# Output projection of two heads by plain products, with reciprocals in one transfer and the value exchange on SP

## The chip, the cores and the metric

The kernel runs on one core of a Trainium2 chip. The metric is the device time of one execution in microseconds. Engines are named as in the profile: PE (TensorE's matmuls), PEld (its weight loads), DVE (VectorE), ACT (ScalarE), POOL (GpSimd), and SP (SyncE, which here only issues DMAs).

## The reference

One transformer layer: layer norm, attention of 16 heads of 128 over 2048 tokens of width 256, and a feed-forward part with ternary weights, added up with the input. Cut to what matters:

```python
qkv = einsum('bsd,ed->bse', xn, Wqkv)               # 16 heads of 128, S = 2048, dim = 256
logits = einsum('bqhd,bkhd->bhqk', q, k) * 128 ** -0.5
w = softmax(logits)
out = einsum('bhqk,bkhd->bqhd', w, v).reshape(B, S, H * D)
y = einsum('bse,de->bsd', out, Wout)                # the output projection: all heads summed
x = x + y + ffn(xn)
```

Everything is float32. An fp32 matmul is two instructions in the profile; a product of a 128 x 128 weight with 512 columns is issued in two halves of 64 rows (`in_halves`), so it is four instructions.

## The kernel before, in words

After a lead-in of some 130 us (layer norm, the feed-forward part, first keys, queries and values) the kernel runs over 64 blocks `n`: 16 heads `h`, and for each four blocks `b` of QB = 512 queries. A block has four steps `t`, one for each 128 queries. Heads come in groups `g` of G = 2, so a group has GB = 8 blocks. All instructions of one step are issued in an order written out by hand (the loop from L1031); each engine keeps that order.

In the step of index `u = 4n + t`:

- `scores` (L610) computes the scores of a step `v = u + 6`, that is six steps ahead (16 PE instructions in two PSUM tiles). DVE takes their maxima (L630, L633), ACT the exponentials (L640) into the tiles `p`.
- `exchanged` (L646) sends `p` from SBUF to SBUF, into the tiles `part`, in 16 DMAs: ten are issued by SP, six by ACT (L659). With 32 x 32 transposes on DVE (L706, two steps later, in `transposed`) that turns the exponentials around. The tiles `p` and `part` are few, so an exponential waits for an older exchange to land, and an exchange waits for an older transpose.
- `differences` (L711, L726) forms sums and differences of the turned exponentials on POOL, and `weighted` (L755, L773) multiplies them with the values. Values times exponentials and other products here use seven block products in place of eight (Strassen's scheme), with the extra additions on POOL and DVE. `v_combined` (L742, L748) forms the sums of the values, once a head, on POOL.
- `copied` (ACT, L791) and `added` (DVE, L799) put the result of a block together in `oU`. At the end of a block `added` multiplies `oU` with the reciprocals of the sums into `oT` (L801). `put_away` (L827), the first thing that POOL does in the next block, stores `oT` in DRAM (`ods`).
- The reciprocals come from `inverses` (L664, in step 2 of the block before): sum, reciprocal and a transpose on DVE, then four DMAs on POOL into a row of DRAM (`rds`, L678). `spread` (L682, L685, step 1 of the block) reads that row back into all partitions, in `oT`.

Beside that, products for the other heads and groups are put into the same steps. In steps 2 and 3: keys and queries of a later head (`fast_product`, `fast_read`, L163 to L217, tiles `pw`), and `fast_scaled` (L219), which makes one query block out of a key block by a scaling on DVE (L223), once in two blocks. In steps 0 and 1 of the first four blocks of a group: the output projection of the two heads of the group before (`fast_o_product`, tiles `pow`). In steps 0 and 1 of the last four blocks: the values of the next group (`fast_v_product`, tiles `pvw`). A first product stands behind the scores; when `twice` is set, a second one stands behind the weighting, and DVE reads it at the start of the next step. All these products share one PSUM bank (tag `m`), so each waits until DVE has read the one before.

The projection before takes two query blocks and two heads at a time: `o_fetched` (L834) loads what was put away into `o3`, `o_difference` (L841) forms differences on POOL, `sums_of` the sums of weights, and seven products a pair of blocks are read by DVE into the sums `osums`, each into one to four places (L911). `y_moved` (L837) brings the sums of a block from DRAM (`yds`) and back. `o_moved`, `o_begun` and `o_loaded` say in which block and step each of these stands.

The values of the next group are turned around too: `v_sent` (L317, four DMAs into DRAM, `vds`), `v_landed` (L324, two DMAs back into `v_part`), `v_transposed` (L328, L331, two transposes on DVE). For the first head of the next group `v_sent` stands in step 0 of the sixth and eighth blocks of a group, `v_landed` in step 1, `v_transposed` in step 2; for the second head in steps 2, 3 and, with a step or more between, in the block after. All those DMAs are issued by POOL. `between` (L988) is called at the end of a step, behind that step's exchange, and holds most of this order.

Of the kernel before, what the change touches and what calls it, by code (L numbers as in the profile page):

```python
# [20 lines left out]
def layernorm_attention_bitffn_kernel(  # L21
# [206 lines left out]
    o3 = const.tile([P, 3, QB], F32, tag="o3", name="o3")  # L228
# [88 lines left out]
    def v_sent(h: int, half: int):  # L317
# [3 lines left out]
        for q in range(P // 32):  # L321
            nc.gpsimd.dma_start(vd[q], v[bass.ts(q, 32)].rearrange("r (j c) -> r j c", c=S // 8))

    def v_landed(half: int):  # L324
        for u in range(2):
            nc.gpsimd.dma_start(v_part[u], vds[half][:, bass.ts(u, QB)])

    def v_transposed(h: int, half: int):  # L328
# [335 lines left out]
    def inverses(n: int):  # L664
# [12 lines left out]
        for j in range(P // 32):  # L677
            nc.gpsimd.dma_start(  # L678
                rds[n % 2][:, bass.ts(j, 32)], riT[32 * j : 32 * j + TB, :]
            )  # L680
# [112 lines left out]
    def added(n: int, r: int):  # L793
# [6 lines left out]
        if r == 3 and n < NBK - NB:  # L800
            nc.vector.tensor_tensor(oT, u, rbs[n], ALU.mult)  # L801
# [22 lines left out]
    def put_away(n: int):  # L824

        h, b = blocks[n]
        nc.gpsimd.dma_start(ods[h % (2 * G)][b], oT)  # L827
# [6 lines left out]
    def o_fetched(g: int, pair: int, i: int, head: int, c: int):  # L834
        nc.gpsimd.dma_start(o3[:, i], ods[(g * G + head) % (2 * G)][2 * pair + c])

    def y_moved(pair: int, c: int, back: bool):  # L837
        y, yd = osums[:, c], yds[2 * pair + c]
        nc.gpsimd.dma_start(*((yd, y) if back else (y, yd)))

    def o_difference(i: int, a: int, b: int):  # L841
        nc.gpsimd.tensor_tensor(o3[:, i], o3[:, a], o3[:, b], ALU.subtract)  # L842

    def o_loaded(g: int, i: int):
        if i % 2 == 0:
            y_moved(i // 2, 0, False)

    def o_moved(g: int, i: int, t: int):

        pair, more = i // 2, i == 1  # L850
        at = i % 2, t
        if at == (0, 0):
            o_difference(1, 2, 1)
        elif at == (0, 1):
            o_difference(0, 1, 0)
        elif at == (0, 2):
            o_fetched(g, pair, 2, 1, 0)
        elif at == (1, 0):
            o_difference(2, 2, 1)
            if more:  # L860
                o_fetched(g, 1, 0, 0, 0)
        elif at == (1, 1):
            y_moved(pair, 1, True)
        elif at == (1, 2):
            if more:
                y_moved(1, 1, False)
                o_fetched(g, 1, 1, 0, 1)
            else:
                y_moved(pair, 0, True)
        elif at == (1, 3) and more:  # L870
            y_moved(pair, 0, True)
            o_fetched(g, 1, 2, 1, 1)
            o_difference(1, 1, 0)

    def o_begun(g: int, i: int, t: int):

        at = i, t
        if at == (6, 2):
            o_fetched(g, 0, 0, 0, 0)
        elif at == (6, 3):  # L880
            o_fetched(g, 0, 1, 0, 1)
        elif at == (7, 1):
            o_difference(1, 1, 0)
        elif at == (7, 2):
            o_fetched(g, 0, 2, 1, 1)

        if at == ((6, 3) if g else (7, 2)):
            y_moved(0, 1, False)

    def o_parts(g: int, m: int):  # L890
        w = weights[g, "o"]
        k, q = w[:, :, :P], w[:, :, P:]
        s = wxs[f"wos{g}"]
        k0, k1, q0, q1 = (0, 0), (1, 0), (0, 1), (1, 1)
        return (
            ((s[:, 0], 1, (k1, q1)), (s[:, 3], 2, (k1,))),
            ((k[:, 0], 0, (k1, q1, k0, q0)),),
            ((s[:, 2], 0, (q0, q1)), (k[:, 1], 2, (k0,))),
            ((s[:, 1], 1, (k1, q0, q1)), (q[:, 1], 2, (q0,))),
        )[m % NB]  # L900

    def fast_o_product(g: int, m: int, second: bool):
        lhs, i, _ = o_parts(g, m)[second]
        pm = ps_m.tile([P, QB], F32, tag="m", name=f"pow{g}_{m}_{int(second)}")
        in_halves(pm, lhs, o3[:, i], True, True)
        return pm

    def fast_o_read(g: int, m: int, second: bool, pm):
        for c, e in o_parts(g, m)[second][2]:
            y = osums[:, c, e]  # L910
            nc.vector.tensor_tensor(y, pm, y, ALU.add)  # L911

# [75 lines left out]
    def between(n: int, t: int):  # L988
# [14 lines left out]
        if g and i < NB:  # L1003
            o_moved(g - 1, i, t)
        elif n < last:
            o_begun(g, i, t)
# [4 lines left out]
        if n >= last - 1 and t == (1 if n < last else 2):  # L1011
            b = n + 1 - last
            nc.gpsimd.dma_start(o3[:, b % 2], ods[(H - 2) % (2 * G)][b])
# [189 lines left out]
```

## Time and profile before

| what | before |
|---|---|
| median of 3 runs | 2299.64 us (2299.03 to 2301.24) |
| the profiled execution | 2299.23 us |
| its span, first to last instruction | 2297.5 us, granted TensorE clock 0.992 |
| busy PE / DVE / POOL / ACT | 95% / 82% / 77% / 32% of the span |
| DMA | 398.46 MB, mean 173 GB/s; exchange 2556 issues on SP, 1540 on ACT |
| median from issue to landing | exchange 2.2 us (SP), 2.5 us (ACT); values out 3.6 us, values in 5.2 us (POOL) |

In the groups of the profile a row gives line, engine, operation, tiles and shapes, then the count, the busy time in us and the mean of one in ns, and behind the second bar the idle time of the engine ahead of them and what ended it. In a timeline a row gives the start and the length in us, the engine, the line, the operation, the tiles and the count; brackets give the idle time ahead and what ended it. Rows of SPq and ACTq are issues of DMAs. Matmuls are pipelined: one of 128 x 512 is shown as 594 ns, and the next may start after some 213.

### The profile page before, as it was taken

What the parts mean: (1) busy time and instruction counts of PE and PEld (TensorE: products, weight loads), DVE (VectorE), ACT (ScalarE), POOL (GpSimd) and SP (SyncE); (2) the same over time, 40 slices, a digit from 0 to 9 for tenths busy, and PEclk for the clock granted to TensorE, in tenths of its full rate; (3) what the DMA queues carried; (4) which work ended last, traced back from release to release, by engine and by line L of the source; (5) the groups of instructions that cost most, each with busy time, mean ns of one, the idle gap of its engine ahead of it and who ended that gap; (6) DMA issues with size and microseconds to landing.
All of it is one profiled execution on the core that took longest, in us unless ns stands there. A gap on an engine that the chain in (4) does not pass through costs nothing.

```text
span 2297.5 us, 41411 instructions
## 1 busy us (share of the span) xinstructions
PE 2189.6 (95%) x13514; PEld 1094.3 (48%) x13514; DVE 1887.3 (82%) x2562; ACT 744.9 (32%) x1390; POOL 1765.6 (77%) x1376
## 2 busy tenths in 40 slices
PE   9999999999999999899998999999999999999898
PEld 6744444454445444455444544444444544445455
DVE  6577888888788888789888888888888788888764
ACT  5543332333232323323333233332333233323331
POOL 0167878887788887988788887888789788898773
PEclk9999999999999999999999999999999999999999
DMA  2166667676676767776677766767677676776764
GB/s 89 55 151 155 150 179 196 166 208 158 175 205 173 189 161 190 193 193 184 162 184 187 199 175 174 198 173 191 159 183 210 171 185 161 189 194 184 193 172 123
DMA packets 246568, 398.46 MB, mean 173 GB/s; under 512 B 80720, under 2 KB 85264, under 8 KB 246352
## 3 DMA queue, kind: packets, MB, share of 16 engines
q1 hardware_dynamic: 127664, 174.95, 29.9%
q0 software_dynamic: 43792, 118.93, 18.6%
q10 hardware_dynamic: 74896, 101.94, 17.3%
q8 instruction: 106, 1.74, 0.3%
q14 instruction: 110, 0.90, 0.1%
HBM read 77.66 MB, written 49.41 MB: 55 GB/s over the span
## 4 chain that ended last, share of the span: by engine, by line
PE 28%; POOL 23%; DMA 19%; DVE 14%; issue 7%; SPq 5%; ACT 2%; ACTq 2%; DVEq 0%; POOLq 0%
DMA part<-p 17%; POOL R L726 14%; PE s L94 10%; PE av L773 8%; SPq L659 5%; DVE mx L630 4%; DVE R L706 3%; POOL st L748 2%; PE ph L508 2%; ACTq L659 2%; ACT p L640 2%; PE pow L94 1%; DVE oU L799 1%; PE pvw L94 1%; PE pw L94 1%
## 5 line engine op out<-in xcount | busy, mean ns | idle before, releaser
L726 POOL TENSOR_TENSOR R<-R 128x1024 f32<-128x1024 f32 x441 | 1181.6, 2686 | 37.0 <-DVE R L706 17.1
L640 ACT ACTIVATE p<-s,nm 128x1024 f32<-128x1024 f32 x512 | 566.2, 1111 | 1381.8 <-DMA part<-p 924.0
L94 PE MATMUL s<-kT,qT 128*64 128x512 f32 x4000 | 946.2, 594 | 13.9 <-ACT p L640 13.7
L630 DVE TENSOR_REDUCE mx<-s 128x1 f32<-128x1024 f32 x512 | 613.1, 1218 | 182.3 <-PE s L94 168.1
L706 DVE STREAM_TRANSPOSE R<-part 128x1024 f32<-128x1024 f32 x512 | 605.2, 1220 | 48.4 <-DMA part<-p 44.9
L94 PEld LDWEIGHTS s<-kT,qT 128*64 128x64 f32 x4000 | 331.1, 137 | 529.0 <-issue 442.1
L773 PE MATMUL av<-R,st 128*64 128x256 f32 x3024 | 495.9, 388 | 53.7 <-POOL R L726 50.2
L773 PE MATMUL av<-R,v 128*64 128x256 f32 x3728 | 539.7, 379 | 0.4 <-DVE oU L799 0.3
L773 PEld LDWEIGHTS av<-R,v 128*64 128x64 f32 x3728 | 341.9, 137 | 186.5 <-issue 56.7
L773 PEld LDWEIGHTS av<-R,st 128*64 128x64 f32 x3024 | 297.7, 139 | 208.1 <-POOL R L726 77.4
L678 POOL DMA_DIRECT2D rd<-r x240 | 124.8, 527 | 162.4 <-DVE r L676 162.1
L827 POOL DMA_DIRECT2D od<-oT x60 | 34.5, 575 | 157.7 <-DVE oT L801 150.2
L799 DVE TENSOR_TENSOR oU<-av,oU 64x256 f32<-64x256 f32 x248 | 101.1, 408 | 54.5 <-ACT oU L791 51.9
L911 DVE TENSOR_TENSOR osums<-pow,osums 128x512 f32<-128x512 f32 x196 | 124.6, 677 | 0.6 <-PE pow L94 0.6
L791 ACT COPY oU<-av 64x256 f32<-64x256 f32 x248 | 91.0, 367 | 94.4 <-PE av L773 90.1
L94 PE MATMUL pw<-t,ws 128*64 128x512 f32 x336 | 109.2, 592 | 0.0
L640 ACT ACTIVATION_READ_ACCUMULATOR p<-s,nm 128x1 f32 x512 | 100.2, 196 | 0.0
L160 POOL TENSOR_TENSOR t<-xnT 128x512 f32<-128x512 f32 x4 | 5.1, 1270 | 107.2 <-DMA part<-p 107.2
L315 DVE TENSOR_TENSOR v<-pvw,v 128x512 f32<-128x512 f32 x98 | 65.1, 676 | 24.9 <-PE pvw L94 24.9
L94 PE MATMUL pw<-xnT,wk 128*64 128x512 f32 x224 | 67.5, 599 | 14.2 <-DVE kT L200 14.2
L200 DVE TENSOR_TENSOR kT<-pw,kT 128x512 f32<-128x512 f32 x112 | 76.9, 686 | 1.8
L842 POOL TENSOR_TENSOR o<-o 128x512 f32<-128x512 f32 x56 | 71.7, 1280 | 0.5
(165 smaller groups left out, 1630.8 us busy)
## 6 DMA issues: line engine op xcount, KB each, us to landing
part<-p SPq DMA_DIRECT2D x2556, 64.0 KB, 2.2
part<-p ACTq DMA_DIRECT2D x1540, 64.0 KB, 2.5
oT<-rd POOLq DMA_DIRECT2D x60, 256.0 KB, 4.3
od<-oT POOLq DMA_DIRECT2D x60, 256.0 KB, 3.6
o<-od POOLq DMA_DIRECT2D x60, 256.0 KB, 4.4
vd<-v POOLq DMA_DIRECT2D x112, 128.0 KB, 3.6
xnT<-vd POOLq DMA_DIRECT2D x56, 256.0 KB, 5.2
osums<-yd POOLq DMA_DIRECT2D x28, 512.0 KB, 6.2
```

The source lines that it names most:

```text
L94: nc.tensor.matmul(out[c * HP : (c + 1) * HP], lhs[:, c * HP : (c + 1) * HP], rhs, start=start, stop=stop, skip_group_check=True,)
L200: nc.vector.tensor_tensor(k, pk, base, ALU.add)
L630: nc.vector.tensor_reduce(mx[:, i : i + 1], s, AX.X, ALU.max)
L640: nc.scalar.activation(p, s, AF.Exp, bias=nm, accum_out=sums[n][:, t, i : i + 1],)
L659: queue.dma_start(parts[v][g // 2][bass.ts(j, 32), g % 2, :], ps[j // 2][bass.ts(g, 32), bass.ts(j % 2, S // NQ)],)
L678: nc.gpsimd.dma_start(rds[n % 2][:, bass.ts(j, 32)], riT[32 * j : 32 * j + TB, :])
L706: nc.vector.transpose(to[:, t % 2, 2 * i : 2 * i + 2], part.rearrange("p g (s c) -> p g s c", s=2),)
L726: nc.gpsimd.tensor_tensor(o, x, y, ALU.subtract)
L773: nc.tensor.matmul(av[i * HP : (i + 1) * HP, half], l[:, kk], moving(s, kk), start=start, stop=(k == units[r] - 1), skip_group_check=True,)
L791: nc.scalar.copy(u[op, oq], av[ap, half])
L799: nc.vector.tensor_tensor(u[p, q], av[p, half], u[p, q], ALU.add)
L911: nc.vector.tensor_tensor(y, pm, y, ALU.add)
```

## The change

The output projection is done with plain products: for each query block and each half of the 256 outputs, one product for each of the two heads, both added up in PSUM, and one sum by DVE. No differences and no weight sums are formed for it. A step does one such pair of products behind the scores, and there is no second one behind the weighting. The two heads of a block lie side by side in DRAM and are fetched by one DMA; the sums of one block are brought while those of the other are in work.

The reciprocals go to DRAM in one DMA of the whole transposed tile, and the spread reads four runs of 128 out of it; the order of the reciprocals in a row differs by that, so the multiplication reads them in another order. It now works in place in `oU`, and `put_away` stores `oU`.

`v_sent` and `v_landed` are issued by SP. The scaling in `fast_scaled` is done by ACT.

```diff
@@ fast_scaled
-        nc.vector.tensor_scalar(q0, k1, SCALE, None, ALU.mult)
+        nc.scalar.activation(q0, k1, AF.Copy, scale=SCALE)
...
-    o3 = const.tile([P, 3, QB], F32, tag="o3", name="o3")
+    o3 = const.tile([P, G, QB], F32, tag="o3", name="o3")
@@ v_sent
-            nc.gpsimd.dma_start(vd[q], v[bass.ts(q, 32)].rearrange("r (j c) -> r j c", c=S // 8))
+            nc.sync.dma_start(vd[q], v[bass.ts(q, 32)].rearrange("r (j c) -> r j c", c=S // 8))
@@ v_landed
-            nc.gpsimd.dma_start(v_part[u], vds[half][:, bass.ts(u, QB)])
+            nc.sync.dma_start(v_part[u], vds[half][:, bass.ts(u, QB)])
@@
-        [away.tile([P, QB], F32, tag=f"od{h}_{c}", name=f"od{h}_{c}") for c in range(NB)]
-        for h in range(2 * G)
+        [away.tile([P, G, QB], F32, tag=f"od{g}_{c}", name=f"od{g}_{c}") for c in range(NB)]
+        for g in range(2)
...
-    rds = [away.tile([TB, P], F32, tag=f"rd{i}", name=f"rd{i}") for i in range(2)]
+    rds = [away.tile([P, 32], F32, tag=f"rd{i}", name=f"rd{i}") for i in range(2)]
@@ inverses
-        for j in range(P // 32):
-            nc.gpsimd.dma_start(
-                rds[n % 2][:, bass.ts(j, 32)], riT[32 * j : 32 * j + TB, :]
-            )
+        nc.gpsimd.dma_start(rds[n % 2], riT)
@@ spread
-            nc.gpsimd.dma_start(oT, rds[n % 2].rearrange("t p -> (t p)").partition_broadcast(P))
+            r = rds[n % 2].rearrange("(j c) r -> j (c r)", c=32)[:, : TB * 32]
+            nc.gpsimd.dma_start(
+                oT.rearrange("p (j x) -> p j x", j=P // 32), r.partition_broadcast(P)
+            )
@@ added
-            nc.vector.tensor_tensor(oT, u, rbs[n], ALU.mult)
+            u = u.rearrange("p (t j r) -> p t j r", t=TB, r=32)
+            r = rbs[n].rearrange("p (j t r) -> p t j r", t=TB, r=32)
+            nc.vector.tensor_tensor(u, u, r, ALU.mult)
@@ put_away
-        nc.gpsimd.dma_start(ods[h % (2 * G)][b], oT)
+        nc.gpsimd.dma_start(ods[h // G % 2][b][:, h % G], oU)
@@ o_fetched, o_difference, o_loaded, o_moved, o_begun, o_parts, fast_o_product, fast_o_read go; new:
+    def o_fetched(g: int, b: int):
+        nc.gpsimd.dma_start(o3, ods[g % 2][b])
+
+    def y_moved(b: int, back: bool):
+        y, yd = osums[:, (b + 1) % 2], yds[b]
         nc.gpsimd.dma_start(*((yd, y) if back else (y, yd)))
+
+    def o_product(g: int, m: int, second: bool):
         w = weights[g, "o"]
+        pm = ps_m.tile([P, QB], F32, tag="m", name=f"pow{g}_{m}")
+        for i in range(G):
+            in_halves(pm, w[:, i, bass.ts(m % 2, P)], o3[:, i], i == 0, i == G - 1)
         return pm
+
+    def o_read(g: int, m: int, second: bool, pm):
+        y = osums[:, (m // 2 + 1) % 2, m % 2]
+        nc.vector.tensor_tensor(y, pm, y, ALU.add)
@@ between
         if g and i < NB:
-            o_moved(g - 1, i, t)
-        elif n < last:
-            o_begun(g, i, t)
+            if t == 0 and i + 1 < NB:
+                y_moved(i + 1, False)
+            elif t == 2:
+                y_moved(i, True)
+                if i + 1 < NB:
+                    o_fetched(g - 1, i + 1)
+        elif n < last and (i, t) == (GB - 1, 2):
+            y_moved(0, False)
+            o_fetched(g, 0)
...
-            if i == GB - 1 and n < last:
-                wo = weights[g, "o"]
-                sums_of(wo[:, :, :P], wo[:, :, P:], f"wos{g}")
@@ the loop
-                    product, read, twice = fast_o_product, fast_o_read, j % NB != 1
+                    product, read, twice = o_product, o_read, False
...
-                if n >= GB and n % GB < NB:
-                    o_loaded(n // GB - 1, n % GB)
```

More of the change, by code (lines that the diff above doesn't have):

```diff
@@ L826, in put_away @@
         h, b = blocks[n]
[L827 to L890, printed above, removed]
-        w = weights[g, "o"]
[L892 to L905, printed above, removed]
-        return pm
[L908 to L911, printed above, removed]
+        nc.gpsimd.dma_start(ods[h // G % 2][b][:, h % G], oU)
@@ L1012, in between @@
             b = n + 1 - last
-            nc.gpsimd.dma_start(o3[:, b % 2], ods[(H - 2) % (2 * G)][b])
+            nc.gpsimd.dma_start(o3[:, b % 2], ods[(H - 2) // G % 2][b][:, 0])
         if g and (i, t) == (0, 1):
```

## The prediction

> **What bounds the kernel now.** I read the page first (busy shares, groups, DMA issues), then the waits, then the timelines of PE, POOL, DVE and SP in and between two groups of heads. From the page:
>
> ```profile
> PE 2189.6 (95%) x13514; PEld 1094.3 (48%) x13514; DVE 1887.3 (82%) x2562; ACT 744.9 (32%) x1390; POOL 1765.6 (77%) x1376
> ...
> L678 POOL DMA_DIRECT2D rd<-r x240 | 124.8, 527 | 162.4 <-DVE r L676 162.1
> ...
> L911 DVE TENSOR_TENSOR osums<-pow,osums 128x512 f32<-128x512 f32 x196 | 124.6, 677 | 0.6 <-PE pow L94 0.6
> ...
> L842 POOL TENSOR_TENSOR o<-o 128x512 f32<-128x512 f32 x56 | 71.7, 1280 | 0.5
> ```
>
> PE is the fullest engine. Its timeline in block 41 (the second of a group, with output products in it) shows it running without a hole:
>
> ```profile
> 1535.32 3.60 PE L94 MATMUL s<-kT,qT 128*64 128x512 f32 x16
> 1538.76 1.03 PE L94 MATMUL pow<-o,wos 128*64 128x512 f32 x4
> 1539.61 3.81 PE L773 MATMUL av<-R,st 128*64 128x256 f32 x32
> ```
>
> A product is four instructions; from its start to the next start is 1539.61 - 1538.76 = 0.85 us. Block 40, the first of the group, does have holes, and POOL's timeline there has none for 40 us:
>
> ```profile
> 1501.58 0.59 PE L773 MATMUL av<-R,st 128*64 128x256 f32 x2
> 1505.31 3.10 PE L773 MATMUL av<-R,st 128*64 128x256 f32 x16 [3.13 <-POOL R L726]
> ```
>
> ```profile
> 1493.45 1.13 POOL L326 DMA_DIRECT2D xnT<-vd  x2
> 1494.58 0.56 POOL L827 DMA_DIRECT2D od<-oT  x1
> 1495.12 0.54 POOL L839 DMA_DIRECT2D osums<-yd  x1
> ```
>
> So the loop is PE-bound with a few holes, and I count those by block. From one multiplication L801 to the next in DVE's timeline is a block. The sixes of a group (n = 6 mod 8) last 32.3 us in the median and the second ones 32.6; I take 32.4 as PE's floor. Over it, summed over the seven groups: first blocks 253.8 - 7 x 32.4 = 27.0 us, third blocks 8.6. The sixth blocks of the six whole groups with value products (n = 5 mod 8) have 1.8 each, the eighth 3.1 each. That is what can be won, and where. The last view is DVE at the eighth block's end and SP's queue beside it:
>
> ```profile
> 1755.16 0.71 DVE L331 STREAM_TRANSPOSE v<-xnT 128x512 f32<-128x512 f32 x1 [1.26 <-DMA xnT<-vd]
> 1756.06 0.71 DVE L331 STREAM_TRANSPOSE v<-xnT 128x512 f32<-128x512 f32 x1 [0.18 <-DMA xnT<-vd]
> ```
>
> ```profile
> 1758.29 1.08 PE L94 MATMUL pw<-xnT,wk 128*64 128x512 f32 x4 [1.51 <-DVE kT L200]
> ```
>
> ```profile
> 1198.76 46.46 SPq L659 DMA_DIRECT2D part<-p  x52
> ```
>
> DVE waits for the landed values, and PE waits 1.51 us for DVE's next read behind them: there a microsecond of DVE is a microsecond of PE. SP issues 52 transfers in 46.46 us with no break the view would part.
>
> **The change, part by part.** The sum starts from the profiled execution, 2299.2 us (span 2297.5); the median of the runs, 2299.6, is 0.4 above, and I carry the sum over as it is. About 0.2%, 4.6 us, can be told from no change.
>
> *Products.* Before, 224 + 168 = 392 instructions make 98 products; after, two for each of 8 steps in 7 groups, 112. 14 x 0.855 = **+12.0 us**, all on the path, since PE has no hole where they go (the second step of first and third blocks).
>
> *POOL's and DVE's share of the output.* Gone are 56 differences (71.7 us of POOL), four weight sums a group (0.47 each, 1.9), four fetches a group (0.57 each), and of 196 sums on DVE 140 (140 x 0.677 = 95 us of DVE). Most of this is beside PE. On the path is the chain that starts with put-away L827, which waits for DVE's multiplication (POOL waits 150.2 us for it, 44 times, so in most blocks POOL was early and its relief is worth nothing). In block 40 it was 2.2 us late; without the work before it, it starts 0.3 us after the multiplication's end, at 1492.7. Then 0.56 + 4.82 + 2.52 + 2.35 (put-away, differences, value sums, half of T2; the fetch of y, 0.54, is gone) puts the half at 1502.95 and, with 0.55 for a y load and 2.4, the other half at 1505.9. PE arrives 0.86 later by its extra product and 0.58 earlier without its wait for the first read, at 1501.9: waits of 1.1 and 1.2 where it had 3.5, 1.8 and 0.58. Won: 3.6 us. The same in block 24, where the put-away was on time: 4.2 before, 2.6 left, won 1.6. With four blocks like 24, 48 worse than 40 (5 us) and 56 at 1.3 that is 17 us. In third blocks PE waited 0.6 to 1.5 us for L911; one product and one read a step end that: 7 us. Together **-24** (between -14, if only the excess of blocks 40 and 48 goes, and -36, all of 27.0 + 8.6).
>
> *Reciprocals.* Four issues (4 x 0.527) become one. The nearest row for its 128 pieces is 0.57. The broadcast has four runs a partition now; its issue costs between 0.57 as before and 4 x 0.57; the weight load with two runs took 0.72, so I take about 1. POOL wins a microsecond a block and is early in most: **-3** (0 to -6), in blocks 0 to 7, where it is late at t = 1. The multiplication reads in runs of 32 and now works in place; 0.69 alone before, and the permuted sums L200 take 0.69 too: 0. The nearest permuted row with a longer time is L223, 1.46; 60 x 0.77 = 46 us of DVE would be the other end, but that row is slow for another reason:
>
> *The scaling of q0* leaves DVE (28 x 1.463 = 41 us) for ACT. Its 28 times are 1.29 or 1.60 us but for one of 0.43; POOL's differences run beside the slow ones. [...] By the rows: PE's weight loads waited 13.9 us for L197 behind it, 27 times, most under the 0.4 us of other gaps; I take **-6** (0 to -14). ACT gets 28 x 0.60 (row L132) at the head of a step, waiting for DVE's k sum; the exps are queued behind, and ACT was idle 1381.8 us before exps: hidden.
>
> *oU instead of oT.* ACT's next copy into oU now waits until the put-away has landed. From the multiplication's end to that copy are 5.6 us in the median; the issue comes 0.3 later and lands after 3.65. The margin is negative in 11 of 60 blocks, by 2.0 at most. Behind the copy are six exchange issues and two exps, and PE needs the copy only after 16 score instructions (3.4) and a product: 0; if that cover is gone, +8 (11 blocks by 0.7).
>
> *Values by SP.* 24 issues a group leave POOL (16 x 0.565 and 8 x 0.557) and go behind SP's exchange. Price on SP: 0.42 (its loads at the start) to 0.59 (an exchange issue), so four sends take 1.7 to 2.4 us, and the ten exchange issues of the next step, the two loads and all later exchanges stand behind them. DVE needs the loads one step after, in the sixth and eighth blocks: 14 places. POOL issued them on average 4.0 us before SP ended the exchange of that step (0.4 to 8.8 us in the 14). So SP's loads start 4.0 + 1.9 = 5.9 later. They land faster: 5.2 now by POOL, 2.2 for an exchange piece of 64 KB by SP; I take 3.2, so 2.0 is won back. And the ten issues, which took 6.4 us in calm steps and up to 12.4 here, no longer share the engines with the loads: I take 1.9. Left: 2.0 us a place, and PE's wait grows with it: **+28**. Ends: -15 (DVE's present waits at L331, 10.3 + 4.7, go) and 14 x 3.9 = +55 (nothing won from sharing). [...]
>
> Sum: 12 - 24 - 3 - 6 + 28 = +7, so **2306 us**.
>
> **The rivals.** *SP has room* (faster). SP's own waits include 100.3 us for DVE's transposes L706, 87 times: there it is ahead, as with 2.7 us just before the exchange at 1687. If the sends fall into such gaps and contention takes the rest, the values cost 3 us instead of 28: 12 - 24 - 3 - 6 + 3 = -18, 2281. It decides below 1.5 us a place, where the other terms' -21 is used up (21 / 14). Against it: DVE waits for these loads already.
> *SP becomes the bound.* 12 more issues in the sixth and eighth blocks at 0.59 are 7.1 us, of which its gaps take about 3.0; 14 x 4.1 = 57 in place of 28: +36, 2335. For it: exchange groups there already follow each other after 0.1 us in most steps. Against: transposes have 2 to 8 us between landing and use.
> *They cancel*: within 4.6 us, 2299. The parts do what they say: nothing suggests that a part is without effect on the program.
>
> **How the numbers follow.** Slower as summed 0.42, SP as the bound 0.12, SP with room 0.38, cancelling 0.08. Slower is 0.42 + 0.12 = 0.54. The range: the faster case spreads from 2264 to 2294, the bound one from 2320 to 2355; leaving out the lowest fifth of the one and most of the other's upper half gives 2270 to 2334. The summed case alone is 2304 to 2318.
>
> **What would show it.** Right: pow at 448 instructions with a matmul time near 0.594 each; L911's successor 56 times; PE's waits for POOL R halved in first blocks (about 2.4 us each left); blocks of first and third kind near 34.8 and 33.4; DVE's wait at the value transposes (now 15 us) near 40, with PE's pw wait for DVE kT grown by as much; sixth and eighth blocks longer by 2. Wrong: value waits on DVE unchanged or less (then SP had room), exps late and PE's scores waiting for ACT (then SP is the bound), or ACT's copies waiting for put-aways while PE waits for them (the oU cover was not there).

## The result, and the profile after

The changed kernel takes 2478.12 us in the median of 4 runs (2460.64 to 2481.69), the kernel before 2300.14 beside it: a ratio of 1.0763, with a 95% interval from 1.0724 to 1.0802. The prediction was 2306. The side was right and the size was not: 178 us more, where 7 were forecast. The profiled execution took 2478.82 us (span 2477.0, granted clock 0.958 where it was 0.992).

First the page of the changed kernel, its busy line and groups (before: PE 2189.6, POOL 1765.6; 240 stores of reciprocals, 196 sums):

```profile
PE 2224.6 (90%) x13570; PEld 1088.2 (44%) x13570; DVE 1776.7 (72%) x2394; ACT 762.8 (31%) x1418; POOL 1491.8 (60%) x916
...
L677 POOL DMA_DIRECT2D rd<-r x60 | 33.5, 559 | 256.4 <-DVE r L676 256.4
L331 DVE STREAM_TRANSPOSE v<-xnT 128x512 f32<-128x512 f32 x56 | 37.4, 692 | 134.5 <-DMA xnT<-vd 95.9
...
L94 PE MATMUL pow<-o,wo 128*64 128x512 f32 x448 | 105.6, 592 | 0.2 <-DVE qT L197 0.2
```

What the change meant to do, it did: 448 product instructions, 60 stores, POOL relieved by 274 us and DVE by 111 us. But the value transposes L331, whose waits were 15 us, now wait 134.5, and PE is idle where it was not. The waits of PE, with the total, the number and the longest:

```profile
PE pw L94 <- DVE kT L200: 146.5, 25, 13.3
PE pw L94 <- DVE qT L197: 41.9, 14, 6.3
PE s L94 <- ACT p L640: 28.6, 17, 5.9
PE av L773 <- POOL R L726: 20.3, 21, 3.1
```

Before, the same four were:

```profile
PE av L773 <- POOL R L726: 50.2, 41, 4.1
PE pw L94 <- DVE kT L200: 14.2, 13, 3.1
PE s L94 <- ACT p L640: 13.7, 11, 6.1
PE pw L94 <- DVE qT L197: 1.1, 4, 0.6
```

So POOL's lateness went down by 30 us, as meant, and two new waits of 132 and 41 us came. They have their places. The length of a block, from multiplication to multiplication (L801 before, L803 after), is the mean over the blocks 8 to 59:

| block of the group | 1 | 2 | 3 | 4 | 5 | 6 | 7 | 8 |
|---|---|---|---|---|---|---|---|---|
| before, us | 36.3 | 33.1 | 33.6 | 33.3 | 34.5 | 34.2 | 32.2 | 35.5 |
| after, us | 37.2 | 37.2 | 36.1 | 35.2 | 34.0 | 39.6 | 33.5 | 45.1 |

The sixth and eighth blocks, those with the value exchange, take most of it: 109 of the 183 us by which the blocks n = 1 to 59 got longer. One eighth block end in the timelines of SP, DVE and PE:

```profile
984.96 10.10 SPq L659 DMA_DIRECT2D part<-p  x15
995.10 7.03 SPq L322 DMA_DIRECT2D vd<-v  x4
1002.30 9.88 SPq L659 DMA_DIRECT2D part<-p  x10
1012.23 1.08 SPq L326 DMA_DIRECT2D xnT<-vd  x2
1013.47 4.95 SPq L659 DMA_DIRECT2D part<-p  x8
```

```profile
1015.34 1.35 DVE L331 STREAM_TRANSPOSE v<-xnT 128x512 f32<-128x512 f32 x2 [11.89 <-DMA xnT<-vd]
...
1017.46 0.69 DVE L200 TENSOR_TENSOR kT<-pw,kT 128x512 f32<-128x512 f32 x1
```

```profile
1002.73 3.60 PE L94 MATMUL s<-kT,qT 128*64 128x512 f32 x16
1018.21 1.97 PE L94 MATMUL pw<-xnT,wk 128*64 128x512 f32 x4 [11.88 <-DVE kT L200]
```

Read from the top: the four sends take SP 7.03 us (1.7 to 2.4 were forecast), the ten exchange issues of the next step start behind them and take 9.88, the loads are issued at 1012.23. DVE stands idle for 11.89 us at the transposes. PE's next product needs the PSUM bank that DVE's read L200 frees, which stands behind them: 11.88 us. And that product then takes 1.97 us instead of 1.08. The reason for that is in the windows of the same stretch (columns: window, length, PE's busy time and count, granted clock, DMA share, GB/s):

```profile
1000.00:1005.00 5.00, 5.00 (x36) 1.00 0.99 285
1005.00:1010.00 5.00, 1.33 (x8) 0.92 0.85 250
1010.00:1015.00 5.00, 0.00 (x0) 0.50 0.66 182
1015.00:1020.00 5.00, 1.79 (x6) 0.50 0.50 132
1020.00:1025.00 5.00, 5.00 (x28) 0.72 0.59 145
```

The granted clock is 0.50 in the window in which PE is idle throughout and in the one after it; PE works again from 1018.21, and in the last window the clock is still 0.72 in the mean. So the stall costs more than its length here: PE's busy time grew by 35.0 us (2224.6 - 2189.6), and only 12 of these, by the prediction's estimate, are the added products.

The second stall, DVE's wait for the scaling, is seen at the end of a third block, in ACT's, DVE's and PE's timelines:

```profile
827.71 6.50 ACTq L659 DMA_DIRECT2D part<-p  x6
834.26 0.63 ACT L223 ACTIVATE qT<-kT 128x512 f32<-128x512 f32 x1 [10.53 <-DMA part<-p]
```

```profile
834.93 0.69 DVE L197 SCALAR_TENSOR_TENSOR qT<-pw,qT 128x512 f32<-128x512 f32 x1 [6.73 <-ACT qT L223]
```

```profile
835.67 1.98 PE L94 MATMUL pw<-t,wq 128*64 128x512 f32 x4 [6.34 <-DVE qT L197]
```

ACT issues six pieces of the exchange, which take it 6.50 us, and the scaling comes behind them.

Last, the products. Where block 40, the first of a group, had holes, POOL now gets to PE's reads in time (the put-away, two groups of differences, the value sums), and in PE's timeline a step's pair of products is eight instructions, 1.7 us from start to start:

```profile
1626.47 0.58 POOL L829 DMA_DIRECT2D od<-oU  x1 [5.59 <-DVE oU L803]
1627.07 4.83 POOL L726 TENSOR_TENSOR R<-R 128x1024 f32<-128x1024 f32 x2
1631.85 1.27 POOL L748 TENSOR_TENSOR v<-v 128x512 f32<-128x512 f32 x1
```

```profile
1627.68 1.88 PE L94 MATMUL pow<-o,wo 128*64 128x512 f32 x8
1629.39 3.62 PE L773 MATMUL av<-R,v 128*64 128x256 f32 x32
```

### The profile page after: what moved, and what is told of

It is laid out like the page before. It is cut to its first block, busy times and chain, and to the rows that moved or that the text cites. A ratio compares the mean times of both kernels' runs of the same rounds, so it can differ in the third digit from the quotient of the medians.

```text
span 2477.0 us, 40829 instructions
## 1 busy us (share of the span) xinstructions
PE 2224.6 (90%) x13570; PEld 1088.2 (44%) x13570; DVE 1776.7 (72%) x2394; ACT 762.8 (31%) x1418; POOL 1491.8 (60%) x916
## 4 chain that ended last, share of the span: by engine, by line
PE 41%; DMA 29%; SPq 9%; POOL 6%; DVE 6%; issue 4%; ACTq 3%; ACT 2%; DVEq 0%; POOLq 0%
DMA part<-p 27%; PE av L773 14%; PE s L94 13%; SPq L659 9%; POOL R L726 4%; PE pw L94 3%; ACTq L659 3%; DVE R L706 3%; PE pvw L94 3%; PE pow L94 2%; PE ph L508 2%; DMA xnT<-vd 1%; POOL st L748 1%; ACT p L640 1%; PE pf L531 1%
## 5 line engine op out<-in xcount | busy, mean ns | idle before, releaser
L94 PE MATMUL s<-kT,qT 128*64 128x512 f32 x4000 | 942.3, 601 | 28.6 <-ACT p L640 28.6
L773 PE MATMUL av<-R,v 128*64 128x256 f32 x3728 | 555.0, 391 | 1.4 <-DVE oU L799 1.3
L773 PE MATMUL av<-R,st 128*64 128x256 f32 x3024 | 472.1, 381 | 23.0 <-POOL R L726 20.3
L829 POOL DMA_DIRECT2D od<-oU x60 | 34.2, 569 | 341.2 <-DVE oU L803 340.1
L94 PE MATMUL pw<-xnT,wk 128*64 128x512 f32 x224 | 76.9, 718 | 135.4 <-DVE kT L200 135.3
L677 POOL DMA_DIRECT2D rd<-r x60 | 33.5, 559 | 256.4 <-DVE r L676 256.4
L331 DVE STREAM_TRANSPOSE v<-xnT 128x512 f32<-128x512 f32 x56 | 37.4, 692 | 134.5 <-DMA xnT<-vd 95.9
L94 PE MATMUL pw<-t,ws 128*64 128x512 f32 x336 | 99.7, 595 | 11.2 <-DVE kT L200 11.2
L94 PE MATMUL pow<-o,wo 128*64 128x512 f32 x448 | 105.6, 592 | 0.2 <-DVE qT L197 0.2
L94 PEld LDWEIGHTS pw<-xnT,wk 128*64 128x64 f32 x224 | 17.4, 154 | 173.4 <-DVE kT L200 152.7
L197 DVE SCALAR_TENSOR_TENSOR qT<-pw,qT 128x512 f32<-128x512 f32 x84 | 57.8, 688 | 42.5 <-ACT qT L223 41.7
```

What stands on the lines that cost most here:

```text
L94: nc.tensor.matmul(out[c * HP : (c + 1) * HP], lhs[:, c * HP : (c + 1) * HP], rhs, start=start, stop=stop, skip_group_check=True,)
L197: nc.vector.scalar_tensor_tensor(q, pm, SCALE, base, ALU.mult, ALU.add)
L773: nc.tensor.matmul(av[i * HP : (i + 1) * HP, half], l[:, kk], moving(s, kk), start=start, stop=(k == units[r] - 1), skip_group_check=True,)
```

## The experiments

The theory: the four parts cost what they cost mainly through transfers. The DMAs of SP and ACT hold each other up, the values come late, and the scaling stands in the same line. The rivals were that one part is the cause of all (the broadcast in short runs, or the scaling), or that the crowded queue makes the exponentials late. Times of the kernel before vary by chip and run between 2288.95 and 2306.99 us, so each result is given as a ratio to the runs of before on its own chip, with its 95% interval, and in us as that ratio less one, times 2300.

### Taking parts out of the change

**Values by POOL again**, all else as changed:

```diff
-            nc.sync.dma_start(vd[q], ...)
+            nc.gpsimd.dma_start(vd[q], ...)
...
-            nc.sync.dma_start(v_part[u], vds[half][:, bass.ts(u, QB)])
+            nc.gpsimd.dma_start(v_part[u], vds[half][:, bass.ts(u, QB)])
```

> The changed kernel with the value exchange (its 16 sends and 8 loads a group) issued by POOL again; all else as changed. Theory A (the sends wait on SP in the queue of transfers, the loads come late, DVE waits for them and PE for DVE): PE's wait for DVE's kT, 146.5 us in the changed kernel and 14.2 before, falls below 25, the sixth and eighth blocks come back from 39.6 and 45.1 us to within 1 us of 34.2 and 35.5, and 2478 falls by 110 to 135 us, to 2343 to 2368. Rival B (the broadcast of the reciprocals in four runs of 512 bytes crowds the DMA engines, and the values are only late because of that): DVE's waits at the value transposes stay above 60 us in sum, and the time stays above 2400. Rival C (the scaling on ACT makes q late, and all else follows): the time falls by less than 60 us.

Measured: 2337.89 us, ratio 1.0181 (1.0154 to 1.0209), that is +42 instead of +175.5. The sixth and eighth blocks take 35.1 and 36.8 us, PE's wait for kT is 38.8. So the values are 134 us of the 175, a little over what theory A gave. B and C are out as causes of the whole. The wait for kT didn't fall as far as expected; 24 us of it belong to another part (the broadcast, below: with products alone and the old broadcast this wait is 14.6).

**Scaling by DVE again**, all else as changed:

```diff
-        nc.scalar.activation(q0, k1, AF.Copy, scale=SCALE)
+        nc.vector.tensor_scalar(q0, k1, SCALE, None, ALU.mult)
```

> The changed kernel with the scaling of q0 on DVE again (28 tensor_scalar), the value exchange still by SP. Theory A (the scaling stands on ACT behind six exchange issues of its step that wait for transfers; DVE's q sum waits for it and PE for that): PE's wait for DVE's qT, 41.9 us in the changed kernel and 1.1 before, falls below 8, the time by 30 to 45 us, to 2433 to 2448, and the sixth and eighth blocks stay at 39 and 45 us. Rival B (ACT's lateness is only the values' lateness passed on): the time stays within 10 us of 2478. Rival C (giving DVE its 28 instructions back costs what it wins): PE's wait for DVE's kT grows by the same 40 us.

Measured: 2446.29 us, ratio 1.0650 (1.0614 to 1.0685), +149.5: the scaling is 26 us here (32 by the medians). The sixth and eighth blocks stay at 38.7 and 44.9. PE's wait for qT fell from 41.9 to 17.1, not to 8: DVE's own scalings stand in front of the q sums again (in the trace, in each of these 12 waits one is among the four instructions ahead). The wait for kT stayed at 144.3, so rival C is out. Theory A, with that correction.

**Both back**: only products and one transfer of the reciprocals remain.

> The changed kernel with both the values on POOL and the scaling on DVE again: what remains is plain products, one transfer of the reciprocals and its broadcast in four runs. If the two costs add up (132 for the values, 40 for the scaling): 2300 to 2315. If they overlap (each hides a part of the other): 2280 to 2300. By the prediction's own terms for these two parts, 12 - 24 - 3 = -15 against 2300: 2285. If the broadcast in short runs costs by itself, the time stays above 2310 and the second to fourth blocks of a group stay 2 to 4 us longer than before.

Measured: 2323.51 us, ratio 1.0116 (1.0076 to 1.0155), +27. Above the additive 2300 to 2315, so another part costs. The second and third blocks are 34.9 and 34.2, the fourth 33.0: the second is longer by 1.8 and the third by 0.6, less than the 2 to 4 of that alternative. PE's wait for kT is 40.0.

**Products alone**: as the last one, and the reciprocals as before.

```diff
-        nc.gpsimd.dma_start(rds[n % 2], riT)
+        for j in range(P // 32):
+            nc.gpsimd.dma_start(
+                rds[n % 2][:, bass.ts(j, 32)], riT[32 * j : 32 * j + TB, :]
+            )
...
```

> The changed kernel with values on POOL, scaling on DVE and the reciprocals in four transfers with their contiguous broadcast: only the plain products (and the put-away from oU) remain of the change. The prediction's terms for the products are 12 - 24 = -12: 2288 (between -14 and -36 for the second term, so 2276 to 2298). If the broadcast in runs of 512 bytes is a cost of its own, this run is 15 to 40 us under the one with it; if it is free, the two agree within 5 us. If PE's 14 added products are all that counts: 2312.

Measured: 2311.06 us, ratio 1.0057 (1.0036 to 1.0079), +13. The number is that of "PE's 14 added products are all that counts", but the blocks say something else: first and third blocks are no longer than before although each has a product more (36.1 and 33.4), and the second blocks, where no product is added, are 37.0 instead of 33.1: 27 us in the seven groups. In POOL's, ACT's and PE's timelines of a second block:

```profile
736.41 0.59 POOL L839 DMA_DIRECT2D yd<-osums  x1
737.00 0.54 POOL L835 DMA_DIRECT2D o<-od  x1
737.55 4.82 POOL L726 TENSOR_TENSOR R<-R 128x1024 f32<-128x1024 f32 x2
```

```profile
738.64 7.42 ACTq L659 DMA_DIRECT2D part<-p  x6
746.16 1.11 ACT L640 ACTIVATE p<-s,nm 128x1024 f32<-128x1024 f32 x1 [7.55 <-DMA part<-p]
```

```profile
747.42 3.68 PE L94 MATMUL s<-kT,qT 128*64 128x512 f32 x8 [3.61 <-ACT p L640]
```

The change sends the sums of a block to DRAM and fetches the next two heads in the same step, 512 KB each, one right behind the other. The store lands after 4.5 us, the fetch after 7.5. The exchange pieces that ACT issues beside them take it 7.42 us, the next exponential is late, and PE's scores wait 3.61 us. Before, a step held 512 and 256 KB of these transfers at most; the two such pairs in the trace of before near that place landed 4.6 and 5.7 us after the second one's issue. Taking the two apart was tried next.

**Products alone, the store a step later:**

```diff
-            elif t == 2:
-                y_moved(i, True)
-                if i + 1 < NB:
-                    o_fetched(g - 1, i + 1)
+            elif t == 2 and i + 1 < NB:
+                o_fetched(g - 1, i + 1)
+            elif t == 3:
+                y_moved(i, True)
         elif n < last and (i, t) == (GB - 1, 2):
-            y_moved(0, False)
             o_fetched(g, 0)
+        elif n < last and (i, t) == (GB - 1, 3):
+            y_moved(0, False)
```

> Products alone, with one edit: the sums of a block go back to DRAM in step 3 of the block instead of step 2, and the first block's sums are brought in step 3 of the group's last block instead of step 2, so that the 512 KB fetch of the two heads (step 2) no longer stands right behind another 512 KB transfer. Theory D (the 12 us that the plain products cost over the kernel before come from these 1 MB in one step: exchange pieces behind them land after 5 to 7 us and the scores of the second block wait for ACT): the second blocks of a group fall from 37.0 us to under 34, PE's wait for ACT's p from 30.7 us to under 18, and the time to 2285 to 2298. Rival E (the products simply cost their 12 us of PE, and the relief of POOL is worth nothing): 2306 to 2314, unchanged.

Measured: 2290.59 us, ratio 0.9969 (0.9954 to 0.9984), -7. The fetch now lands in a median of 5.1 us instead of 7.4, the second blocks fall to 34.8, and PE's wait for ACT to 18.6 (both a little above the 34 and 18 expected):

```profile
PE av L773 <- POOL R L726: 37.3, 31, 3.8
PE s L94 <- ACT p L640: 18.6, 14, 4.1
```

Theory D: one edit that takes the two transfers of a step apart gave 20 us back, and the plain products are then a small gain.

### Single parts on the kernel before

**Values by SP alone** (the two lines of the first diff, the other way round):

> The kernel before with one edit: the value exchange is issued by SP instead of POOL. Theory A (the queue of transfers on SP and ACT is the cost, whatever else is changed): DVE waits 5 to 12 us at the value transposes of each sixth and eighth block, PE as long for DVE's kT, and the time is 2300 plus 90 to 135, so 2390 to 2435. Rival B (SP has the room; it is the other parts of the change that fill it): within 15 us of 2300. The prediction's own term for this part, +28: 2328.

Measured: 2424.68 us, ratio 1.0555 (1.0523 to 1.0587), +128. Theory A. The sixth and eighth blocks take 39.1 and 43.5 us. PE's wait for kT, and DVE's timeline in the eighth block of the second group:

```profile
PE pw L94 <- DVE kT L200: 122.9, 16, 11.8
```

```profile
702.77 0.71 DVE L331 STREAM_TRANSPOSE v<-xnT 128x512 f32<-128x512 f32 x1 [8.52 <-DMA xnT<-vd]
703.80 0.71 DVE L331 STREAM_TRANSPOSE v<-xnT 128x512 f32<-128x512 f32 x1 [0.32 <-DMA xnT<-vd]
```

**Sends alone, loads alone by SP:**

> The kernel before with only the 16 sends a group (v_sent) issued by SP; the 8 loads stay on POOL. Theory F (what costs is the order on SP: the sends wait there for landed pieces, the exchange of the next step stands behind them, and the loads behind that): the sends land 4 to 11 us later than by POOL, the exchange of the next step is 3 to 6 us late, the loads are issued by POOL once the sends have landed: the wait of DVE at the value transposes is 1 to 4 us a place, the time 2320 to 2365. Rival G (only the loads' place matters, the sends are free): 2295 to 2310.

> The kernel before with only the 8 loads a group (v_landed) issued by SP; the 16 sends stay on POOL. By the prediction's own figures the loads are issued 4.0 us later, at SP's end of the step's exchange, and land 2.0 us faster: 2.0 a place of 14, so 2300 plus 28 = 2328 (2315 to 2340); DVE waits about 2 us a place at the transposes. Rival G: nearly all of the 125 us of both together, 2390 or more. Theory F: both halves together cost more than the sum of each alone.

Measured: loads alone 2325.53 us, ratio 1.0110 (1.0084 to 1.0137), +25, as the prediction's figures gave it (DVE waits 50.7 us at the transposes, 3.6 a place where 2 were expected). Sends alone 2419.55 us, ratio 1.0520 (1.0496 to 1.0544), +120, far above what either theory allowed. DVE's waits at the transposes are short there (30.2 us for the loads); the lateness came out elsewhere. POOL issues the loads, must wait for the sends to land, and its differences R stand behind that in its queue. POOL's and PE's waits:

```profile
POOL xnT L326 <- DMA vd<-v: 164.2, 40, 10.6
```

```profile
PE av L773 <- POOL R L726: 99.0, 44, 6.5
PE pw L94 <- DVE kT L200: 52.4, 12, 8.1
```

Sends that come late thus cost about the same whether DVE or POOL is the one that stands waiting for what follows them (128 and 120 us). With both halves on SP the cost is less than the sum of the two (128 against 145): theory F failed there too.

**One send in place of four.** Why four sends are so dear: their number, or their place behind the exchange? Values are stored as they lie in SBUF, which takes one DMA of 512 KB, and four loads of 128 KB turn them around:

```diff
-        for q in range(P // 32):
-            nc.gpsimd.dma_start(vd[q], v[bass.ts(q, 32)].rearrange("r (j c) -> r j c", c=S // 8))
+        nc.sync.dma_start(vds[half], v)
...
-        for u in range(2):
-            nc.gpsimd.dma_start(v_part[u], vds[half][:, bass.ts(u, QB)])
+        c = S // 8
+        for q in range(P // 32):
+            vd = vds[half][bass.ts(q, 32)].rearrange("r (j c) -> j r c", c=c)
+            nc.gpsimd.dma_start(v_part[q // 2][:, bass.ts(q % 2, c)], vd)
```

> The kernel before with values sent in one DMA of 512 KB instead of four of 128 KB (stored as they stand in SBUF) and loaded in four DMAs of 128 KB instead of two; the send is issued by SP, the loads by POOL. Theory I (what costs is the number of issues: each waits on SP until an older transfer has landed): one issue in place of four takes 1 to 1.5 us instead of 4 to 6 of SP's time, and of the 120 us that four sends by SP cost alone less than 50 remain over the same layout by POOL. Theory K (what costs is the place: the send starts only behind the step's exchange, 5 to 10 us later than POOL starts it, and POOL waits for it with its loads): more than 80 of the 120 remain.

> The control: the same layout (one send, four loads), all issued by POOL. POOL issues five instead of six, the loads in runs of 1 KB instead of 2 KB: within 15 us of 2300, 2295 to 2315.

Measured: 2355.92 us, ratio 1.0255 (1.0223 to 1.0286), +59, with the send on SP; 2318.29, ratio 1.0088 (1.0059 to 1.0116), +20, with it on POOL, 3 us above the range expected of this control. The difference is 38 us where four sends made it 120: some two thirds go with four issues in place of one, as theory I has it. The one send also writes longer runs into DRAM (4 KB in place of 1 KB), and no run tells that from the number. The rest goes with the place, or with the larger transfer, which no run tells apart either. Where four cost more can be seen in the traces: in the eighth blocks SP starts the exchange of the send's step 3.9 us after the end of its exponentials with four sends by SP, 0.6 with one and 0.6 before (means over seven groups). With four, SP still has the delay of the sixth block there. SP's timeline around a send in such an eighth block, first of this kernel, then of the one with four sends by SP; from the send on, the two take about the same time (18.8 and 19.3 us), so the difference lies ahead of these rows:

```profile
956.21 0.46 SPq L320 DMA_DIRECT2D vd<-v  x1
956.78 18.20 SPq L659 DMA_DIRECT2D part<-p  x20
```

```profile
969.66 3.60 SPq L322 DMA_DIRECT2D vd<-v  x4
973.42 15.53 SPq L659 DMA_DIRECT2D part<-p  x20
```

**Values by SP, more room in the sixth and seventh blocks:**

```diff
-            (5, 0): (v_sent, 0, 0), (5, 2): (v_transposed, 0, 0), (6, 1): (v_transposed, 1, 0),
+            (5, 0): (v_sent, 0, 0), (5, 3): (v_transposed, 0, 0), (6, 2): (v_transposed, 1, 0),
...
-        if i in (5, 7) and t % 2 and g + 1 < H // G:
-            v_landed(i // 2 - 2)
+        if (i, t) in ((5, 1), (6, 0), (7, 1), (7, 3)) and g + 1 < H // G:
+            v_landed(int(i == 7))
```

> The kernel before with the whole value exchange by SP, and in the sixth and seventh blocks of a group more room: DVE's value transposes of the first head in step 3 instead of step 2, the loads of the second head in step 0 of the seventh block instead of step 3 of the sixth, its transposes in step 2 instead of step 1. The eighth block and what follows it are left as they were, as a control. Theory F (SP's transfers come some 5 us late in the sixth block, and that is time only because DVE's transposes follow one step after the loads): the sixth blocks fall from 39.1 us to 34 to 35.5, the eighth stay at 43 to 45, the time is 2425 less 7 x 4 = 28 to 40, so 2385 to 2397. Rival H (the crowded queue itself makes PE late, through the exponentials): the sixth blocks stay above 37.5, and the time above 2410.

Measured: 2382.13 us, ratio 1.0365 (1.0332 to 1.0399), +84, 44 less than without the room. The sixth blocks fall from 39.1 to 32.8 us, below the 34.2 of before and the 34 to 35.5 expected; 1.5 us of that come back in the seventh. The eighth, left alone, stay at 43.0. In DVE's timeline the sixth block's transposes have no wait in brackets any more, the eighth's do:

```profile
622.22 1.26 DVE L331 STREAM_TRANSPOSE v<-xnT 128x512 f32<-128x512 f32 x2
...
693.56 0.71 DVE L331 STREAM_TRANSPOSE v<-xnT 128x512 f32<-128x512 f32 x1 [7.33 <-DMA xnT<-vd]
```

Theory F here: in the sixth block SP's sends and loads are as late as without the room (loads landed 24.8 and 24.9 us after the exponentials), and cost it nothing where no one asks for the values one step later. Rival H is out.

**Scaling by ACT alone:**

> The kernel before with one edit: the scaling of q0 is done by ACT instead of DVE. Theory A (ACT's place behind its exchange issues is late by itself): PE's wait for DVE's qT rises from 1.1 us to 25 or more, and the time is 2315 to 2340. Rival B (ACT is only late where the values on SP have made the exchange late): PE's wait for qT stays under 8 us and the time is 2290 to 2305; the prediction's term, -6, gives 2294.

Measured: 2301.06 us, ratio 1.0007 (0.9990 to 1.0024): no difference. Rival B by the time, though PE's wait for qT, 11.1 us, is above the 8 it allowed. DVE waits 17.5 us for ACT's scaling; that what DVE is rid of (its busy time falls from 1887.3 to 1852.7 us) makes up for these waits is likely and was not tested by itself. With products and one transfer in, but values by POOL, the same edit costs 15 us (42 - 27); with values on SP as well it costs 26. What the scaling costs thus grows with the lateness of the exchange pieces in front of it: ACT waits 139.6 us for them ahead of the scaling here and 150.1 in the changed kernel, and DVE waits for the scaling 17.5 and 41.7 us.

**One transfer of the reciprocals alone**, with its broadcast in four runs a partition:

> The kernel before with one edit: the reciprocals go to DRAM in one transfer, are broadcast from there in four runs of 512 bytes, and the multiplication reads them in their new order in place. Theory A (the short runs take the DMA engines' time and delay the exchange pieces behind them): landing of the broadcast grows from 4.3 to about 6 us, SP's wait for landed pieces grows, the time is 2310 to 2340. Rival B (the transfers have time to spare; POOL wins three issues a block): 2290 to 2300, the prediction's term being -3.

Measured: 2316.33 us, ratio 1.0080 (1.0057 to 1.0103), +18: theory A. SP's waits for landed exchange pieces are 345.9 us, 300.5 before. Landing of the broadcast and PE's first wait (4.3 us and 14.2 before):

```profile
oT<-rd POOLq DMA_DIRECT2D x60, 256.0 KB, 5.9
```

```profile
PE pw L94 <- DVE kT L200: 41.5, 16, 5.0
```

The broadcast is the same 256 KB, in runs of 512 bytes instead of 2 KB. It stands in step 1, and so do the loads of the values, which land later by 0.9 and 2.1 us in the sixth and eighth blocks (worked out from the trace); DVE waits 1.3 and 1.8 us longer at their transposes there, and PE behind it.

**One transfer in the order of rows**, the rest as products alone:

```diff
+        nc.gpsimd.dma_start(rds[n % 2].rearrange("c j r -> j c r"), riT)
...
+            nc.gpsimd.dma_start(oT, rds[n % 2][:TB].rearrange("t j r -> (t j r)").partition_broadcast(P))
```

> The changed kernel with values on POOL and scaling on DVE, and the reciprocals in one transfer that writes them in the order of rows, so that the broadcast reads one run of 2 KB a partition and the multiplication reads plainly; the one transfer writes 128-byte runs as before. If the short runs of the broadcast are a cost, this is as fast as the kernel with products alone or up to 5 us faster (POOL wins three issues a block): 2270 to 2290. If they are free, it agrees within 3 us with the kernel that has both parts back and the broadcast in four runs.

Measured: 2312.72 us, ratio 1.0062 (1.0039 to 1.0085), +14, the same as products alone, while the broadcast in short runs is at +27. PE's wait for kT is 16.5 us here and 40.0 there. So the short runs cost some 13 us, and the one transfer itself is free. (The absolute range missed because products alone did.)

**The two mended parts together**, the later store and the order of rows:

> The same edit on the kernel with the reciprocals in one transfer in the order of rows. If the two are independent (the one transfer in row order gave plus or minus 3 us): the time of products alone with the later store, within 4 us, so 2283 to 2298 by theory D; by rival E 2306 to 2316.

Measured: 2285.99 us, ratio 0.9937 (0.9916 to 0.9959), -14. This is faster than both kernels: the change without its two moves to SP and ACT, with a plain broadcast, and with the store a step later.

## Why the prediction was right and wrong

| term | predicted, us | measured alone, us |
|---|---|---|
| products, +12 and -24 | -12 | +13; with the store a step later -7 |
| one transfer of the reciprocals | -3 | +18 |
| scaling to ACT | -6 | +2 (no difference) |
| values to SP | +28 | +128 (loads 25, sends 120) |
| sum | +7 | +161; the whole change +175.5 |

**Values to SP: the step that failed.** The mechanism was the one forecast (loads late, DVE waits at L331, PE waits for kT), the size wasn't. The working was 4.0 us for the place behind the exchange, + 1.9 for four sends, - 2.0 for the faster landing, - 1.9 because "the ten issues ... no longer share the engines with the loads". Three of these terms can be read off the kernel with only the values on SP, counted from the end of the exponentials of the step of the first send (means over seven groups):

| | before, sixth / eighth | values by SP, sixth / eighth |
|---|---|---|
| SP ends the exchange of the send's step | 7.9 / 8.8 | 7.4 / 10.5 |
| next exchange starts | 8.2 / 8.9 | 11.7 / 16.1 |
| it ends | 16.3 / 17.8 | 19.6 / 23.6 |
| loads issued | 12.7 / 13.4 | 19.7 / 23.6 |
| loads landed | 19.6 / 20.0 | 24.9 / 28.0 |

The place: the loads were issued 3.6 and 4.4 us before the exchange ended, 4.0 was right. The landing: 1.7 and 2.2 us faster, 2.0 was right. (The medians say the same: values in took 5.2 us by POOL before and 3.3 by SP in the changed kernel.) Wrong were the other two: the end of the exchange did not move by 1.9 - 1.9 = 0 but by 3.3 and 5.8 us. From the end of one exchange to the start of the next, with the four sends between, are 4.3 and 5.6 us (0.3 and 0.1 before), not 1.9; in the eighth blocks SP was 1.7 us late already; and the exchange behind got shorter by 0.2 and 1.4 us, not by 1.9. Sends were priced by the length of an issue, 0.42 to 0.59 us, but in these steps issues of SP and ACT often start only when an older transfer has landed: of the 112 sends in the kernel with only the values on SP 26 waited for one, 35 us in all. In the trace of before the exchange DMAs of both engines signal on eight semaphores between them; of 4088 issues none starts before the transfer that last used its semaphore has landed, and never more than 8 are under way. With 16 pieces a step, and a step of about 8.5 us of which SP's ten issues take 8.1 to 8.9 in these blocks, there was no gap for four more. The view of SP that the prediction showed (52 issues in 46.46 us with no break) said that; one rival set the pauses of SP before DVE's transposes against it and took them for room.

So the +28 is about what the loads alone cost (+25), and the term that failed is the sends, which the sum had at a net 0 and which cost +120 alone.

From the lateness to the time there was a second step: "PE's wait grows with it". The loads land 5.3 and 8.0 us later, 6.7 on average. But 128 / 14 is 9.1 a place. PE's wait for kT grows by 108.7 us (122.9 - 14.2), 7.8 a place, 1 us more than the lateness, and that 1 us stays unexplained. The rest is seen in the trace as the halved clock after the stall: with the values alone on SP it holds for 177 us in all, before for 39, and PE's busy time grows by 20 us, 1.4 a place. That the sends are the greater part of the cause, and four of them dearer than one, and for the sixth blocks that the short distance of the transposes is the condition, is shown by the runs. The wait for landed transfers is read from the trace; it was not taken away by itself.

**Scaling: "hidden" was the wrong word.** ACT's 1381.8 us of idle time before the exponentials were taken as room. Most of it (924.0 us in the waits of before) is put down to exchange transfers, which ACT's own issues stand and wait for, and the scaling has to stand in the same queue. Alone it costs what it saves (+2 us, no difference); with the other parts of the change in, PE's wait for qT is 41.9 us, 11.1 alone.

**One transfer.** The prediction priced the issue (about 1 us; it takes 0.78) and not the transfer. The landing of the broadcast, 5.9 instead of 4.3 us, was the term left out.

**Products.** The +12 and the -24 were together of the right size: with the store a step later the part is at -7, where -12 was forecast. Neither was measured by itself, and the 17 us of the first blocks are 16.3 by the figures given there. Missing was what is moved along with it: 1 MB of transfers in one step, 20 us. The prediction counted the fetches only as POOL's issue time. PE's waits for POOL's R went down from 50.2 to 20.3 us, more than the "halved" of the forecast, but the first blocks of the changed kernel are 37.2 us and not 34.8, since other waits took their place.

**oU: 0** was right. In the kernel with products alone ACT waits 13.3 us for put-aways, and PE's wait for ACT's copies is 2.2 us, 3.2 before.

**The rivals.** "SP becomes the bound" had the right mechanism with 57 us, less than half of what came. Its condition ("exps late and PE's scores waiting for ACT") is not where the time went: PE's scores waited 28.6 us for ACT, 13.7 before, and most of PE's new waiting is for DVE (kT and qT, 173 us more). All rivals priced the four issues by their length, so none could reach the result, and the range ended at 2334.

## What to carry to other kernels

Before moving DMAs to another queue, count how many that queue has under way and what each issue waits for; where issues follow the landing of older ones, an added DMA can cost more than its issue time (here 26 of 112 sends waited, 35 us in all), and one large send cost less than four small ones (38 us against 120). Look at the consumer's distance first: the same late transfers cost the sixth block 39.1 - 32.8 = 6.3 us or nothing, by one step of order. And ask what an "idle" engine's queue waits for before an instruction is put there: ACT had 1381.8 us of idle time ahead of its exponentials, and the scaling behind its exchange issues cost 26 us in the changed kernel.

## What the runs showed of the hardware that was not expected

- In the traces of before and of the changed kernel the 4096 exchange DMAs that SP and ACT issue signal on eight semaphores between them, and never more than 8 are under way; four sends, 1.7 to 2.4 us by the lengths of issues, took SP 7.03 us in one of the busiest steps of the changed kernel, and 3.2 us in the mean of the 28 places with the values alone on SP.
- In the changed kernel the granted clock is 0.50 in 28 records; all but the last are multiples of 3.41 us long and start 2.1 to 5.4 us after PE fell idle. They make 210 us, 39 before. A product of four instructions took 1.97 us at this clock, in the stall above, instead of 1.08.
- The broadcast of 256 KB in four runs of 512 bytes a partition landed in 5.9 us in the median (one transfer alone, and the changed kernel), in one run of 2 KB in 4.3 (before).
- The 512 KB fetch right behind a 512 KB store landed in 7.4 us in the median (products alone; 7.0 in the changed kernel), with the store a step later in 5.1.
